# Other steps for raw weight loads, projection rows and one attention half in an attention and feed-forward block on one Trainium2 core

## The chip, the cores and the metric

The kernel runs on one core of a Trainium2 chip. The metric is the device time of one execution in microseconds (us); the time before is the median of three runs. The engines are named as in the profile: PE (TensorE, matrix products; PEld are its weight loads), DVE (VectorE), ACT (ScalarE), POOL (GpSimd) and SP (SyncE, which here issues nearly all transfers).

## What is computed

The input x is 4 sequences of 1024 rows of 512 numbers. Each row is normalised, and the result goes into an attention with decaying weights and into a feed-forward part; both are added to x. Cut to what matters:

```python
xn = _layernorm(x)
# attention: 16 heads of 32, in chunks of T = 128 rows
h = _rmsnorm(xn, qkv_norm_w, eps)
q, k, v = split(h @ _weight_quant(qkv_w).T)
def step(S, qkv_c):
    scores = einsum('bhtd,bhsd,hts->bhts', qi, ki, mask)
    intra = einsum('bhts,bhsd->bhtd', scores, vi)
    cross = einsum('bhtd,ht,bhde->bhte', qi, lam_t, S)
    kv = einsum('bhtd,ht,bhte->bhde', ki, lam_rev, vi)
    return lam_T * S + kv, scale * (intra + cross)
out = _rmsnorm(_rmsnorm(outs, norm_w, 1e-6), proj_norm_w, eps) @ _weight_quant(proj_w).T
# feed-forward, hidden size 2048
gated = silu(xn @ w_gate.T) * (xn @ w_up.T)
x = x + out + gated @ w_down.T
```

`_weight_quant` rounds the weights of the attention to -1, 0 and 1 times a scale that is taken from the mean of their absolute values.

## The kernel before

The 4096 rows are worked on in 8 blocks of 512. Every float32 factor is split into two float16 parts (high and low), so one product is three matmuls. The feed-forward part of block 0 (`ffn0`) prepares the weights as it goes and stores the float16 parts in `gu_d` and `wd_d` in the chip's main memory; block 1 reads them back plainly (`ffn_up`, `load_next` L919); blocks 2 to 7 compute the gate and up products with seven block products in the place of eight (`up_seven`). For these, sums and differences of the raw weights' quarters are needed; `up_sums(i)` makes them once, for i from 0 to 15 (two kinds, gate and up, of eight weight groups).

The feed-forward part is a generator; each `yield` is a step, and 48 steps (`TS`) make a block. The attention runs beside it in 14 + 2 halves of 256 rows: `at[n]` is the step at which half n begins, one every 22 steps, and each of its own `yield`s is placed after one feed-forward step. So PE's order is the order in which the program text emits, and alternates between a feed-forward piece and an attention piece. In a half the first four steps make queries and keys (`psa<-h,wqkT`), the next two the values (`psa<-wvT,h`); after two empty steps come the scores (`pss<-qst,kst`), their products with the values (`psa<-x,t`), the cross terms (`psa<-Sst,qst`) and the state (`psa<-t,kn`); four steps later the projection (`psa<-wpT,x`, 28 steps after the half's begin).

Other engines' work is put into lists by due step (`later`, run by `run_due`) and runs in written order: from step 45 on, `in_order` binds DVE, ACT, POOL and SP each to the order of emission. Before that a scheduler of the framework orders them.

What the change and the steps of the prediction touch:

- `up_sums` L1051: at its step it loads two raw tiles of 256 KB (L1060, `t<-in_w_gu_dram`); two steps later POOL makes four sums (L1070); three and four steps later ACT splits each tile (L1075) and DVE the low part one step on (L1077); five and six steps later SP stores both (L1083, `gu_d<-x`, two transfers of 128 KB for each tile). `sums_at` holds the 16 steps.
- `att_half` with `spread`: queries and keys go through main memory: a store (L634, `sd<-qhl`, `sd<-khl`), then three loads (L643, into `qst` or `kst`) which wait for the store; the keys are also transposed (L637, `kn<-khl`). In steps of the half: query store 2, query loads 3, key store 4, key loads 5; the scores follow at 8.
- `scores` L735: DVE empties the one bank `pss` of the scores. `state` L788: DVE adds the state's bank into `S`. `add_acc` L1142: DVE empties a bank into the accumulator.
- `prep_proj` and `prep_proj_w` (generator `side2`): four tiles of the projection's weights are loaded (L1258), their absolute values summed by ACT and DVE (L297, L299), the scale made (L285 to L293, L332, L333), and each tile turned into -1, 0, 1 (L303, L304 on DVE). It takes one `yield` in each step of its window.
- `moved` and `place`: an estimate of the megabytes moved in each step, by which other transfers (`load_acc`, `load_down`, the stores to `wd_d`, x loads) choose their step inside a window.
- `t32` is a pool of 14 tiles of 256 KB, which raw weights, projection rows and most intermediate results share. PSUM has four banks `psf`, three `psa` and one `pss`.

Of the kernel before, what the change touches and what calls it, by code (L numbers as in the profile page):

```python
# [28 lines left out]
def block_kernel(ctx, tc, x, qkv_w, qkv_nwT, proj_w, proj_nwT, proj_nw, norm_w, s, w_gu, w_down, out):  # L29
# [8 lines left out]
    NB = B * N // HB  # L38
# [21 lines left out]
    def wt(shape, dt, tag, bufs=2):  # L60
        return wk.tile(shape, dt, tag=tag, name=nm(tag), bufs=bufs)
# [28 lines left out]
    def later(steps, *fns, last=False):  # L90

        due[LAST if last else FIRST].setdefault(now[0] + steps, []).extend(fns)

    def run_due(part):
        for fn in due[part].pop(now[0], ()):
            fn()
# [21 lines left out]
    @contextmanager  # L118
    def after(inss):
        with ExitStack() as st:  # L120
            for i in inss:
                st.enter_context(tc.issue_after(i))
            yield
# [41 lines left out]
    def t32():  # L165
        return wt([P, 512], F32, "t32", 14)
# [174 lines left out]
    NG = NJ // 2  # L341
# [100 lines left out]
    def half_scales(hh):  # L442
        gs = slice(hh * NG // 2, (hh + 1) * NG // 2)
        q = wt([P, NG // 2 + 1], F32, "gh2", 1)
        V.tensor_reduce(q[:, 0:1], cg[:, gs], AX.X, ALU.min)
        inverse(c2[:, hh : hh + 1], q[:, 0:1], 1 / XS)
        V.tensor_scalar(q[:, 1:], icg[:, gs], q[:, 0:1], XS, ALU.mult, ALU.mult)
        V.tensor_tensor(bsc[:, gs], bsc0[:, gs], q[:, 1:], ALU.mult)
# [143 lines left out]
    def make_h(b, half):  # L592

        xT = blk[b][0]
        hsl = slice(half * UT, (half + 1) * UT)
        h = wt([P, 2, CC, UT], F16, "h", 1)
        blk[b][1] = h
        th = [t32().rearrange("p (c t) -> p c t", c=2) for _ in range(2)]
        for cp in range(2):
            cs = slice(2 * cp, 2 * cp + 2)  # L600
            G.tensor_tensor(th[cp], xT[:, 0, cs, hsl], xT[:, 1, cs, hsl], ALU.add)

        def split(cp):
            for c in range(2 * cp, 2 * cp + 2):
                t, w = th[cp][:, c % 2, :], nwT[:, c : c + 1]
                A.activation(h[:, 0, c, :], t, AF.Copy, scale=w)
                later(int(b > 0), lambda c=c, t=t, w=w: low(c, t, w), last=True)

        def low(c, t, w):
            V.scalar_tensor_tensor(h[:, 1, c, :], t, w, h[:, 0, c, :], ALU.mult, ALU.subtract)  # L610

        for cp in range(2):
            later(2 + cp if b else 1, lambda cp=cp: split(cp), last=bool(b))
# [437 lines left out]
    def up_sums(i):  # L1051

        g, kind = divmod(i, 2)
        w, ts_ = [], []
        o = om[:, g, kind : kind + 1]

        def load():
            for r in range(2):
                w.append(t32())
                SY.dma_start(w[r], w_gu[2 * g + r, kind])  # L1060

        def sums():
            (a11, a12), (a21, a22) = ([t[:, f * UT : (f + 1) * UT] for f in range(2)] for t in w)
            for dst, a, b, op in (
                (a22, a21, a22, ALU.add),
                (a21, a11, a21, ALU.subtract),
                (a11, a22, a11, ALU.subtract),
                (a12, a12, a11, ALU.subtract),
            ):
                G.tensor_tensor(dst, a, b, op)  # L1070

        def split(r):
            t = wt([P, 2 * C], F16, "x16", 9).rearrange("p (f n q) -> p f n q", f=2, n=2)
            wr = w[r].rearrange("p (f q) -> p f q", f=2)
            A.activation(t[:, :, 0, :], wr, AF.Copy, scale=o)  # L1075
            later(
                1, lambda: V.scalar_tensor_tensor(t[:, :, 1, :], wr, o, t[:, :, 0, :], ALU.mult, ALU.subtract), last=True  # L1077
            )
            ts_.append(t)

        def store(r):
            for f, n in enumerate(((1, 6), (2, 3))[r]):
                SY.dma_start(  # L1083
                    gu_d[:, g, kind, n].rearrange("p n c q -> p (n c q)"),
                    ts_[r][:, f].rearrange("p n q -> p (n q)"),
                )

        load()
        later(2, sums, last=True)
        for r in range(2):  # L1090
            later(3 + r, lambda r=r: split(r), last=True)
            later(5 + r, lambda r=r: store(r))

    def ffn_down(b, hh, gts, c):

# [61 lines left out]
    def ffn(b):  # L1157
        for hh in range(2):
            gts = []
            if b == 1:  # L1160
                js = range(hh * NJ // 2, (hh + 1) * NJ // 2)
                done = plain(gts, js[-4])
                for j in js:
                    yield from ffn_up(b, j, gus.pop(NJ * b + j), bsc, done)
            else:
                for g in range(hh * NG // 2, (hh + 1) * NG // 2):
                    yield from up_seven(b, g, gts)
            yield from ffn_down(b, hh, gts, c2[:, hh : hh + 1])

    def ffn0():  # L1170
        prev = None

        def down(ks):
            g, gts = prev
            for k in ks:
                for _ in ffn_down0(0, k, g, gts, icg[:, g : g + 1]):
                    pass

        for g in range(NG):
            nxt = g + 1 < NG  # L1180
            gts = []
            for r in range(2):
                j = 2 * g + r
                for n, _ in enumerate(ffn_up(0, j, gu0.pop(j), bsc0, plain(gts))):
                    stage(6 * g + 3 * r + n)
                    yield
                if g == 0 and r == 0:
                    load_acc(0, 0)
                    load_acc(0, 1)
                stage(6 * g + 3 * r + 2)  # L1190
                if prev is not None and nxt:
                    down((2 * r, 2 * r + 1))
                    yield
            if not nxt:
                down((0, 1))
                yield
                down((2, 3))
                yield
            prev = (g, gts)
        down((0, 1))  # L1200
        yield
        down((2, 3))
        yield
# [60 lines left out]

    TS = 48
    t0 = [TS * b for b in range(NB)]
    at = [round(36 + 22 * n) for n in range(2 * NB - 2)]
    at += [t0[-1] + 4, t0[-1] + 18]
    mh = {max(t0[b], at[2 * b - 1] + 6) if b else at[0] - 3: (b, 0) for b in range(NB)}
    mh.update({at[2 * b] + (4 if b else 7): (b, 1) for b in range(NB)})  # L1270
# [3 lines left out]
    for n in at:  # L1274
        for i, size in ((2, 1.3), (3, 2.0), (4, 1.3), (5, 2.0), (6, 4.0), (24, 2.0), (25, 2.0)):
            moved[n + i] = moved.get(n + i, 0) + size
    sums_at = [t0[1] + 6 + 3 * i if i < 10 else t0[2] + 1 + 4 * (i - 10) for i in range(2 * NG)]
    for n in sums_at:
        for i, size in ((0, 1.3), (5, 0.7), (6, 0.7)):
            moved[n + i] = moved.get(n + i, 0) + size  # L1280
# [6 lines left out]
    for b in range(1, NB):  # L1287
# [3 lines left out]
        for g in range(NG):  # L1291
            hh, n = divmod(g, NG // 2)
# [10 lines left out]
    t = 0  # L1303
    for b in range(NB):
        if b + 1 < NB:
            ln_plan(b + 1, TS)
        for i, _ in enumerate(ffn(b) if b else ffn0()):
            for _ in range(int(0.9 * max(t - 4, 0)) - int(0.9 * max(t - 5, 0))):
                next(side, 1)
            if 44 <= t < 59:  # L1310
                next(side2, 1)
            if t in mh:
                make_h(*mh[t])
            for n, tn in enumerate(at):
                if tn == t:
                    halves.append(att_half(n // 2, n % 2))
            run_due(LAST)
            for hf in list(halves):
                if next(hf, 1) == 1:
                    halves.remove(hf)  # L1320
            t += 1
            now[0] = t
            if t == 6 * NG - 6:
                SY.dma_start(pnw_bc, proj_nw.partition_broadcast(P))
                V.tensor_scalar(pnw_bc, pnw_bc, ps_sc, None, ALU.mult)
            if b == 0 and i == TS - 1:
                with after(pin):
                    half_scales(0)
                    half_scales(1)
            if b == 0 and i == 44:  # L1330
                in_order(keep=False)
            if t in sums_at:
                up_sums(sums_at.index(t))
            run_due(FIRST)
            run_due(LOADS)
            if b or i > 44:
                in_order()
# [56 lines left out]
```

## Time and profile before

| what | value |
|---|---|
| median of three runs | 1302.11 us (1301.87 to 1303.08) |
| the profiled execution | 1303.48 us |
| its span, first to last instruction | 1301.7 us |
| granted TensorE clock, mean | 0.999 |
| scores, PE `pss<-qst,kst` | 512 matmuls, first at 159.8 us |
| half 1's scores, first | 239.1 us |
| raw weights for the sums, L1060 | 32 loads of 256 KB, first at 183.5 us |
| stores of the sums, L1083 | 64 of 128 KB |

The profile shows one execution. Its page gives each engine's busy time, then the chain of work that ended last, then groups of instructions; the trace behind it can be asked for single stretches. A view of waits lists who waited for whom: the total in us, how often, the longest. A timeline row is: start, duration, engine (SPq is SP's queue), line, operation, output and inputs, number of instructions merged, and in brackets the idle time before it and what ended it. A wait for several things is booked to the one that came last by the records, which for a transfer can be its neighbour in the queue.

### The profile page before, as it was taken

The numbers are of one execution on the slowest core, as the hardware profiler recorded it, in microseconds if no ns is written. First come the engines' busy times: TensorE is split into PE (matmuls) and PEld (weight loads), VectorE is DVE, ScalarE is ACT, GpSimd is POOL, SyncE is SP. The second block draws the span as 40 slices with busy tenths as digits, with TensorE's granted clock in tenths as the row PEclk, the third lists the DMA queues.
The fourth block names the chain that finished last, engine by engine and source line by source line (L and its number), as shares of the span: only waits on it lengthen the run. The fifth ranks groups of instructions, "written<-read, shape, count | busy, mean of one in ns | idle before, by whom it ended". The sixth has DMA issues, their size and how long they took to land.

```text
span 1301.7 us, 26358 instructions
## 1 busy us (share of the span) xinstructions
PE 1264.1 (97%) x10242; PEld 864.5 (66%) x10242; DVE 894.4 (69%) x1603; ACT 609.6 (47%) x1160; POOL 780.4 (60%) x846
## 2 busy tenths in 40 slices
PE   5999999999999999999999999999999999999998
PEld 2444455454785867767677685876858678587684
DVE  7898577666767676747866486755858467777573
ACT  6866635355443454434535254443625336344251
POOL 4535547576687585654947278472846546757273
PEclk9999999999999999999999999999999999999999
DMA  9743755978687796938678676866796776958461
GB/s 342 267 160 113 198 150 151 321 257 248 162 262 272 226 258 155 290 124 255 166 184 289 152 238 154 240 226 175 227 190 189 218 203 202 215 168 254 138 167 49
DMA packets 229950, 268.62 MB, mean 206 GB/s; under 512 B 131520, under 2 KB 156096, under 8 KB 229824
## 3 DMA queue, kind: packets, MB, share of 16 engines
q1 hardware_dynamic: 229680, 266.92, 70.7%
q8 instruction: 80, 1.31, 0.4%
q14 instruction: 46, 0.38, 0.1%
q10 hardware_dynamic: 144, 0.01, 0.0%
HBM read 190.85 MB, written 46.14 MB: 182 GB/s over the span
## 4 chain that ended last, share of the span: by engine, by line
PE 70%; DVE 11%; POOL 6%; ACT 4%; DMA 4%; issue 4%; SPq 0%; DVEq 0%; POOLq 0%; ACTq 0%
PE psf L112 51%; PE psa L112 18%; PE pss L112 2%; POOL t L1070 2%; DMA t<-in_w_gu_dram 1%; DVE h L610 1%; DVE t L986 1%; ACT gu L431 1%; DVE acc L1142 1%; DVE t L735 1%; DMA gu<-gu_d 1%; DVE x L1077 1%; DVE ghl L984 1%; POOL t L740 1%; POOL ghl L946 1%
## 5 line engine op out<-in xcount | busy, mean ns | idle before, releaser
L112 PEld LDWEIGHTS <-gu 128*128 128x128 f16 x3936 | 380.5, 98 | 138.6 <-issue 14.4
L112 PE MATMUL psf<-xT,gu 128*128 128x256 f16 (+1 forms) x1920 | 334.3, 317 | 9.9 <-DVE acc L1142 2.8
L112 PE MATMUL psf<-ghl,ghl 128*128 128x512 f16 x1344 | 306.9, 379 | 1.5 <-POOL ghl L946 0.8
L112 PEld LDWEIGHTS <-ghl 128*128 128x128 f16 x1536 | 146.7, 98 | 164.5 <-POOL ghl L946 3.2
L112 PE MATMUL psf<-wda,gu 128*128 128x256 f16 x2016 | 243.6, 273 | 0.2 <-DVE ghl L984 0.2
L740 POOL TENSOR_TENSOR t<-t,t 128x512 f16<-128x512 f32 x128 | 152.7, 1194 | 147.7 <-ACT t L739 145.2
L735 DVE SCALAR_TENSOR_TENSOR t<-pss,rs,mask 128x512 f32<-128x512 f32 x128 | 95.7, 747 | 66.5 <-PE pss L112 62.5
L739 ACT CAST t<-t 128x512 f16<-128x512 f32 x128 | 78.7, 615 | 122.4 <-DVE t L735 120.6
L1045 POOL TENSOR_TENSOR ghl<-ghl,ghl 128x512 f16<-128x512 f32 x96 | 113.9, 1206 | 21.3 <-ACT ghl L1047 21.3
L112 PE MATMUL psa<-h,wqkT 128*128 128x256 f16 x1024 | 122.3, 273 | 1.3 <-DVE S L788 1.3
L984 DVE SCALAR_TENSOR_TENSOR ghl<-psf,bsc,ghl 128x256 f32<-128x256 f32 x192 | 105.0, 547 | 24.6 <-PE psf L112 11.9
L112 PEld LDWEIGHTS <-wqkT 128*128 128x128 f16 x1024 | 99.8, 98 | 18.9 <-DVE S L788 1.4
L986 DVE TENSOR_TENSOR t<-psf,t 128x256 f32<-128x256 f32 x192 | 93.6, 488 | 18.4 <-PE psf L112 9.7
L702 POOL TENSOR_TENSOR t<-t,t 128x512 f16<-128x512 f32 x28 | 33.3, 1190 | 108.7 <-ACT t L701 86.9
L112 PEld LDWEIGHTS <-wda 128*128 128x128 f16 x864 | 82.9, 98 | 12.2 <-issue 1.1
L811 POOL TENSOR_TENSOR t<-t,nw_bc 128x512 f32<-128x512 f32 x32 | 45.8, 1436 | 55.0 <-DVE t L762 55.0
L112 PE MATMUL psf<-xT,wda 128*128 128x256 f16 x576 | 78.5, 272 | 0.0
L1037 POOL TENSOR_TENSOR ghl<-ghl,t 128x512 f32<-128x512 f32 x48 | 63.9, 1331 | 4.1 <-ACT t L1030 2.1
L686 DVE SCALAR_TENSOR_TENSOR x<-psa,rs,x 128x512 f16<-128x512 f32 x32 | 24.0, 751 | 55.3 <-ACT x L683 53.4
L112 PE MATMUL psa<-wvT,h 128*128 128x512 f16 x256 | 60.5, 379 | 1.3 <-DVE S L788 1.3
L1027 ACT ACTIVATE t<-psf,ug 128x256 f32<-128x256 f32 x48 | 22.7, 473 | 80.4 <-DVE t L986 60.8
L834 POOL TENSOR_TENSOR x<-t,x 128x512 f16<-128x512 f32 x30 | 36.1, 1205 | 40.2 <-ACT x L833 40.2
(220 smaller groups left out, 2012.8 us busy)
## 6 DMA issues: line engine op xcount, KB each, us to landing
gu<-gu_d SPq DMA_DIRECT2D x96, 512.0 KB, 4.2
ghl<-wd_d SPq DMA_DIRECT2D x48, 512.0 KB, 4.8
gu<-gu_d SPq DMA_DIRECT2D x48, 384.0 KB, 3.9
wda<-gu_d SPq DMA_DIRECT2D x48, 384.0 KB, 3.6
qst<-sd SPq DMA_DIRECT2D x48, 256.0 KB, 4.2
kst<-sd SPq DMA_DIRECT2D x48, 256.0 KB, 4.2
t<-in_w_gu_dram SPq DMA_DIRECT2D x44, 256.0 KB, 5.0
t<-in_x_dram SPq DMA_DIRECT2D x32, 256.0 KB, 4.5
```

What stands on the lines that cost most here:

```text
L112: tc.keep_in_program_order(nc.tensor.matmul(*a, **k))
L702: G.tensor_tensor(vrl, vr, vrh, ALU.subtract)
L735: V.scalar_tensor_tensor(sm, pss, u.rk, mask[:, 4 * qd : 4 * qd + 4, :], ALU.mult, ALU.mult)
L739: A.copy(smh, sm)
L740: G.tensor_tensor(sml, sm, smh, ALU.subtract)
L811: G.tensor_tensor(o2, o, nw_bc, ALU.mult)
L834: G.tensor_tensor(on[:, 1, :], u.o3, on[:, 0, :], ALU.subtract)
L984: V.scalar_tensor_tensor(dst, src, by, y, ALU.mult, ALU.add)
L986: V.tensor_tensor(dst, src, y, ALU.add)
L1037: later(2, lambda c_=c_: G.tensor_tensor(c_, c_, us[0][4], ALU.mult))
L1045: G.tensor_tensor(lo[:, f], whole[:, f], hi[:, f], ALU.subtract)
L1070: G.tensor_tensor(dst, a, b, op)
```

## The change

Three things are moved; no computation is added or taken away.

1. `sums_at`: the raw weights of `up_sums` 0 to 4 are loaded at steps 52, 54, 56, 58, 67 in place of 54, 57, 60, 63, 66, and those of 14 and 15 at 111 and 115 in place of 113 and 117; the other nine keep their steps. For 14 and 15 everything after the load is due two steps later than before, counted from the load, so it keeps its step. For 0 to 4 the sums, splits and stores move with their load.
2. `prep_proj` runs in the window of steps 38 to 52 in place of 44 to 58.
3. `at[13]`: attention half 13 begins at step 321 in place of 322.

```diff
         load()
-        later(2, sums, last=True)
+        d = 2 if i >= 14 else 0
+        later(2 + d, sums, last=True)
         for r in range(2):
-            later(3 + r, lambda r=r: split(r), last=True)
-            later(5 + r, lambda r=r: store(r))
+            later(3 + r + d, lambda r=r: split(r), last=True)
+            later(5 + r + d, lambda r=r: store(r))
...
-    at = [round(36 + 22 * n) for n in range(2 * NB - 2)]
+    at = [round(36 + 22 * n) - (n == 13) for n in range(2 * NB - 2)]
...
-    sums_at = [t0[1] + 6 + 3 * i if i < 10 else t0[2] + 1 + 4 * (i - 10) for i in range(2 * NG)]
+    sums_at = [t0[1] + (4, 6, 8, 10, 19, 21, 24, 27, 30, 33)[i] if i < 10 else t0[2] + 1 + 4 * (i - 10) - 2 * (i >= 14) for i in range(2 * NG)]
...
-            if 44 <= t < 59:
+            if 38 <= t < 53:
                 next(side2, 1)
```

Half 1 begins at step 58 (58 = 36 + 22), so its key store and key loads fall on steps 62 and 63. Before, the raw weights of sum 3 are loaded at 63 and those of sum 4 at 66; in the changed kernel sum 3 is at 58 and sum 4 at 67. The estimate `moved` follows `sums_at` and `at`, and with it a few of the placed transfers change their step.

## Prediction

> **What bounds the kernel.** I read the totals and the chain of waits first.
>
> ```profile
> span 1301.7 us, 26358 instructions
> PE 1264.1 (97%) x10242; PEld 864.5 (66%) x10242; DVE 894.4 (69%) x1603; ACT 609.6 (47%) x1160; POOL 780.4 (60%) x846
> PE 70%; DVE 11%; POOL 6%; ACT 4%; DMA 4%; issue 4%; SPq 0%; DVEq 0%; POOLq 0%; ACTq 0%
> ```
>
> TensorE (PE) sets the end: of 1301.7 us it is idle for 1301.7 - 1264.1 = 37.6. The change adds and removes no matmul, so it can only open or close holes in PE. Next, what PE waits for; seven lines of that view:
>
> ```profile
> PE psa L116 <- DVE t L468: 9.8, 3, 9.0
> PE pss L112 <- DMA gu<-gu_d: 4.9, 2, 2.6
> PE psf L112 <- DVE acc L1142: 2.8, 1, 2.8
> ...
> PE psa L112 <- DVE S L788: 2.6, 2, 1.3
> ...
> PE pss L112 <- DVE t L735: 1.7, 2, 1.0
> ...
> PE psf L112 <- DMA xT<-x: 0.4, 1, 0.4
> ...
> PE psf L112 <- DMA ghl<-wd_d: 0.3, 1, 0.3
> ```
>
> The 9.8 is the start, untouched. By windows, the rows that the change can reach are: the two score waits of 4.9 in all (at 157-160 and 236-239 us, attention halves 0 and 1), 2.8 at 416-419, one S L788 wait of 1.3 at 1147, xT 0.4 at 169 and ghl 0.3 at 1126. That is 9.7 us, 0.75% of the span; no gain can be larger.
>
> The score waits are booked to gu loads, but scores read qst and kst. The timeline of SP's queue shows the true one:
>
> ```profile
> 221.05 1.28 SPq L643 DMA_DIRECT2D qst<-sd  x3
> ...
> 225.96 1.42 SPq L634 DMA_DIRECT2D sd<-khl  x1
> 227.43 1.04 SPq L1060 DMA_DIRECT2D t<-in_w_gu_dram  x2
> 228.86 0.88 SPq L1083 DMA_DIRECT2D gu_d<-x  x2
> 232.10 1.27 SPq L643 DMA_DIRECT2D kst<-sd  x3
> ```
>
> The key load is issued when the key store has landed (225.96 + 6.1 to landing = 232.1). Its third part, issued at 232.94, takes 6.1 and lands at 239.0, where PE resumes. The raw weights (L1060) stand between store and load.
>
> **The change part by part.**
>
> *Raw weights of sums 14 and 15, two steps sooner: -2.8.* VectorE's (DVE's) timeline at 416:
>
> ```profile
> 408.73 0.41 DVE L761 TENSOR_TENSOR t<-psa,t 128x256 f32<-128x256 f32 x1
> 409.18 0.42 DVE L762 TENSOR_TENSOR t<-psa,t 128x256 f32<-128x256 f32 x1
> 412.68 2.99 DVE L1077 SCALAR_TENSOR_TENSOR x<-t,om,x 128x512 f16<-128x512 f32 x1 [3.08 <-DMA t<-in_w_gu_dram]
> ```
>
> DVE runs in written order; L1077 of sum 14 holds it for 3.08 us, and behind it stand L735, L1077 and the L1142 that PE waits for. The load was issued at 401.21 to 402.06 and takes 7.0. In the new order it stands two places after the gu load of 392.87, at about 394.4, and waits for no engine, so it lands at 394.9 + 7.0 = 401.9. GpSimd (POOL) ends its previous work at 406.2; four sums end at 409.4, ScalarE's 0.72 makes 410.1, against 412.68: DVE gains 2.6, and L1077 probably not 2.99 but nearer the 1.72 of its successor. So the whole 2.8; between -2.6 and -2.8. SP moves past wda, ghl, out, gu and acc transfers: each two transfers of 256 KB later, about 0.67 each at 390 GB/s, 1.3 in all; in 390 to 425 PE waits for none of them. Without that cover the price is up to 1.3. Sum 15 keeps its steps for all but the load, and in the new order both acc loads come before it, so it lands near 414 as now, in time for its sums at 418.2.
>
> *Half 13 one step sooner: -1.3 and -0.3.* At 1146.36 the twelve state matmuls (psa<-t,kn) are followed at once by half 14's first sixteen (psa<-h,wqkT), which wait for the bank that DVE L788 empties (1147.23, 1.16 us). In the new PE order 24 psf matmuls, 2.6 us by this trace's pitch of 0.109, stand between them: the wait goes. New neighbours are the second projection of half 12 and half 13's first scores; DVE's L1142 (0.75) is the only addition there. The last kst part landed at 1109.25 + 6.9 = 1116.2, 0.3 before its scores; these now come one step (2.6) sooner, but the query store no longer stands behind the x transpose of 1094.15 and the key store follows earlier by more than a step, so I take 0; were it not sooner, the price is 2.6 - 0.3 = 2.3. The ghl wait of 0.3 sits behind the kn transposes of the same half and goes too: between -0.3 and 0.
>
> *Raw weights of sums 0 to 4, clear of half 1's keys: -0.95.* What delays the key load is its store's landing, and in the new order the same transfers precede that store, with one more pair of 128 KB stores. Only the time after 232.1 can shrink: first issue to last landing is 6.9 now. The nearest row for the new situation, two small stores ahead and no raw load, is half 3's kst: 379.84, third issue 381.44, plus 4.4 = 385.8, so 6.0. Gain 0.95; the other end is half 13's 7.7 (1108.41 to 1116.1), a loss of 0.8; the best is all of 2.3. The sums themselves move to 181-220 us. Their cover: POOL idles 3.73 and 4.95 us before its L946 at 189.56 and 195.82, and one sum takes 3.4 to 4.1; DVE loses the projection pieces there. Cost 0; if a load came late there, DVE would be held as at 412.68, up to 2.8.
>
> *Projection rows six steps sooner: +1.2 and +1.0.* Here the new order speaks against the change. The four loads (4 x 0.67 = 2.7) now stand before half 0's query store (139.91); half of one gu load (0.67) moves behind it: +2.0 for its landing at 145.2. The query load, the key store and the key load are chained behind it. One kn transpose, whose landing lies 0.8 after the last query load, moves into the wait: 2.0 - 0.8 = +1.2 on the wait of 2.6. The bounds are +2.0 and -1.1: the store's data was through by 142.4 on fifteen of sixteen engines, and an instruction fetch of 1.85 us beginning at 141.4 made the sixteenth 2.3 us late; if that falls elsewhere, 1.2 - 2.3 = -1.1. Taking proj's loads out of 156-167 might close xT's 0.4, but DVE, next, is late there anyway: 0.
>
> [...]
>
> DVE: scores have one bank (pss), and each L735 must empty it before the next scores. At 168-172 DVE is busy 3.82 of 4.00.
>
> ```profile
> 172.71 0.68 DVE L299 TENSOR_REDUCE asum<-t 128x1 f32<-128x512 f32 x1
> 173.42 0.68 DVE L795 SCALAR_TENSOR_TENSOR Sst<-S,Sst 32x512 f16<-32x512 f32 x1
> 174.13 0.75 DVE L735 SCALAR_TENSOR_TENSOR t<-pss,rs,mask 128x512 f32<-128x512 f32 x1
> ```
>
> L735 ends at 174.88; the next scores start at 175.56, a margin of 0.68. In the new order L299 (0.68) is gone from here, and in come the five scale pieces (188.75 to 189.46: 0.71) and one L303 + L304: 0.48 + 0.75 at 195.0, or 0.59 + 1.64 at 197.0. Net 0.71 + 1.23 - 0.68 = 1.26 up to 2.26; less the margin, PE waits 0.6 to 1.6. The mean of L303 + L304 is 1.9, so 1.2; part of the delay runs beside the later kst, and I take +1.0 of 0 to 1.6. At the following scores one more L303 + L304 replaces an L299, and the margin there holds.
>
> The dear row, 1.64, ran beside POOL's L811 and L1070. [...]
>
> *Sum:* -2.8 - 1.3 - 0.3 - 0.95 + 1.2 + 1.0 = -3.15. The profiled execution took 1303.48 (1301.7 of span, 1.8 around it); 1300.3 follows. The median of the runs shown, 1302.11, lies 1.37 lower: 1299.0.
>
> **The rivals.**
>
> A, *the opening is free*: proj's loads and DVE work fit, both +1.2 and +1.0 drop: -5.35, 1296.8. For it: PE had only 0.4 of waits between 160 and 236, and the bounds reach 0. Against: DVE's 3.82 of 4.00.
>
> B, *the keys' load is bound by its store, and the move does not do what it says*: no 0.95 but +0.8, the rest as above: -1.4, 1300.7. For it: the raw loads stand behind the store, not ahead. Against: half 3's row.
>
> C, *slower: the opening pays twice*. The 2.7 of row loads delay the query pair in full and, without a drain, the key pair again; the instruction fetch's 2.3 falls on the second store too, and DVE adds 1.6: 2.7 + 2.7 + 2.3 + 1.6 = 9.3, against the gains of 5.35: +3.95, 1306.1. It decides once the opening costs over 5.35 + 2.6 = 8. For it: query and key transfers are one chain, in one queue. Against: the DMA engines were nearly idle from 142.4 to 146.
>
> **How the numbers follow.** About 0.2%, 2.6 us, is what a measurement of this kernel tells from no change: faster is below 1299.5, slower above 1304.7. Chances: forecast 0.40, A 0.27, B 0.18, C 0.15. The forecast lies 0.5 from the bound; most of its error is on the side of its large, well-founded terms, so 0.32 of its 0.40 is faster: 0.32 + 0.27 = 0.59. Same: 0.08 + 0.18 = 0.26. Slower 0.15. Without C the ends of the bounds are -2.8 - 1.3 - 0.3 - 2.3 - 0.4 - 1.1 = -8.2 and -2.6 - 1.3 + 0.8 + 2.0 + 1.6 = +0.5, or +2.8 with half 13's 2.3. All at an end together is unlikely: 1295.0 to 1304.0 leaves out C and a few in a hundred of A.
>
> **What would show it.** In the profile after: no PE wait for DVE acc near 416; no PE wait for S L788 near 1147, its other one, 1.3 near 1218, unchanged; half 1's first-key-issue to last landing near 6.0 and a score wait of about 1.4 there; the first score wait nearer 3.8 than 2.6; a new PE wait for DVE L735 near 175-178. Wrong would be: the DVE hold by L1077 appearing at another place, a score wait at half 0 under 1.5 or over 6, or any wait over 1 us near 1085-1140.

## The result: slower, and the profile after

| | median, us | executions |
|---|---|---|
| before | 1301.91 (1301.65 to 1303.08) | 5 |
| after | 1308.14 (1306.41 to 1310.41) | 5 |
| after / before | 1.0047, 95% interval 1.003 to 1.0064 | |

The same pair was measured again later, beside more executions: 1306.91 against 1304.02, ratio 1.0026 (1.0015 to 1.0037). So the change costs some 3 us (3.4 by this ratio, 2.9 between the medians), and the 6.2 of the first measurement come in part from a low draw of before, whose medians in four later groups of 17 to 34 executions are 1303.1 to 1304.0. The forecast was 1299.0, faster.

The page of after: its head, the row of PE and the engines' shares of the chain that ended last.

```profile
span 1308.5 us, 26358 instructions
...
PE 1267.8 (97%) x10242; PEld 865.6 (66%) x10242; DVE 892.4 (68%) x1603; ACT 610.0 (47%) x1160; POOL 779.8 (60%) x846
...
PE 74%; DVE 9%; POOL 5%; ACT 4%; DMA 4%; issue 3%; SPq 0%; DVEq 0%; POOLq 0%; ACTq 0%
```

The span grew by 6.8. PE idles for 1308.5 - 1267.8 = 40.7 where it idled for 37.6: 3.1 of the 6.8. The other 3.7 stand in PE's *busy* time, with the same 10242 matmuls: they ran slower. The mean granted clock is 0.994, and was 0.999. Next PE's waits in after (who waited for whom: total in us, times, longest):

```profile
PE pss L112 <- DMA gu<-gu_d: 4.9, 1, 4.9
PE pss L112 <- DVE t L735: 3.3, 4, 1.0
PE psf L112 <- DMA ghl<-wd_d: 3.2, 2, 2.7
...
PE psa L112 <- DVE h L610: 1.4, 2, 1.0
PE psa L112 <- DVE S L788: 1.3, 1, 1.3
```

The total of the first row is that of before, 4.9, but it was two waits and is one: half 0's first scores wait for all of it, half 1's hardly (0.4, booked elsewhere). L735 was 1.7 in two waits and is 3.3 in four. The 2.8 for DVE's acc at 416 is gone, and 3.2 for the down weights (`ghl<-wd_d`) has come, 2.7 of it near 404. One of the two waits for S L788 is gone, and L610 has taken its place. Most of what the change freed came back under another name.

Where the clock went is in the view by windows, cut at the borders of the half-speed stretches that the trace records, which are 3.41 us long or twice that (columns: window, its length, PE busy, granted clock, DMA share, GB/s, with other engines between):

```profile
157.26:160.67 3.41, 1.92 (x9) 0.69 (x7) 3.41 (x7) 2.23 (x5) 1.92 (x2) 1.00 0.79 184
160.67:164.09 3.42, 0.04 (x1) 0.07 (x2) 0.03 (x1) 0.00 (x0) 0.00 (x0) 1.00 0.96 223
164.09:167.50 3.41, 3.41 (x12) 1.48 (x13) 1.81 (x4) 1.66 (x3) 1.16 (x1) 0.50 1.18 293
...
403.02:406.44 3.42, 0.80 (x7) 0.44 (x6) 1.89 (x3) 2.68 (x5) 3.42 (x3) 1.00 1.02 378
406.44:409.85 3.41, 3.29 (x8) 1.16 (x8) 2.13 (x2) 1.88 (x3) 3.04 (x4) 0.50 1.00 305
```

Half 0's score wait leaves the window from 160.67 empty, and in the next PE is granted 0.50: it does in 3.41 us what takes 1.7 at full speed (0.50 x 3.41). The wait near 404 is followed by the same, with 0.80 busy in one window and 0.50 granted in the next. Between the first clock record of its trace, at 20.7, and the last stretch, after has four such windows (27.6, 102.7, 164.1, 406.4); before, from 22.3 on, has one (100.8). Two of the four don't belong to the change: 27.6 lies ahead of all that was moved, and no_rows and rows_loads_far, which are no slower than before, have it too; and after_again, the same kernel once more, has no window near 406, and its longest wait there is 0.7. The one at half 0's scores is there both times.

### The profile page after: what moved, and what is told of

Its sections match the earlier page's. It is cut to its first block, busy times and chain, and to the rows that moved or that the text cites. A ratio compares the mean times of both kernels' runs of the same rounds, so it can differ in the third digit from the quotient of the medians.

```text
span 1308.5 us, 26358 instructions
## 1 busy us (share of the span) xinstructions
PE 1267.8 (97%) x10242; PEld 865.6 (66%) x10242; DVE 892.4 (68%) x1603; ACT 610.0 (47%) x1160; POOL 779.8 (60%) x846
## 4 chain that ended last, share of the span: by engine, by line
PE 74%; DVE 9%; POOL 5%; ACT 4%; DMA 4%; issue 3%; SPq 0%; DVEq 0%; POOLq 0%; ACTq 0%
PE psf L112 54%; PE psa L112 18%; PE pss L112 2%; DMA gu<-gu_d 1%; ACT gu L431 1%; DVE t L735 1%; POOL t L1070 1%; DVE acc L1143 1%; DVE ghl L984 1%; DVE h L610 1%; DVE t L986 1%; DMA t<-in_x_dram 1%; ACT t L435 1%; DMA sd<-qhl 1%; POOL ghl L946 1%
## 5 line engine op out<-in xcount | busy, mean ns | idle before, releaser
L112 PE MATMUL psf<-ghl,ghl 128*128 128x512 f16 x1344 | 310.0, 382 | 4.4 <-DMA ghl<-wd_d 3.2
L735 DVE SCALAR_TENSOR_TENSOR t<-pss,rs,mask 128x512 f32<-128x512 f32 x128 | 95.7, 748 | 73.2 <-PE pss L112 70.2
L112 PEld LDWEIGHTS <-wqkT 128*128 128x128 f16 x1024 | 99.8, 98 | 19.3 <-issue 1.8
L811 POOL TENSOR_TENSOR t<-t,nw_bc 128x512 f32<-128x512 f32 x32 | 45.8, 1436 | 57.1 <-DVE t L762 57.1
L502 DVE TENSOR_TENSOR x<-t,x 128x512 f16<-128x512 f32 x52 | 52.7, 1020 | 11.1 <-ACT x L500 10.8
```

Source lines behind the costliest of these rows:

```text
L112: tc.keep_in_program_order(nc.tensor.matmul(*a, **k))
L502: lambda: V.tensor_tensor(xn2[:, 1, :], src, xn2[:, 0, :], ALU.subtract),
L735: V.scalar_tensor_tensor(sm, pss, u.rk, mask[:, 4 * qd : 4 * qd + 4, :], ALU.mult, ALU.mult)
L811: G.tensor_tensor(o2, o, nw_bc, ALU.mult)
```

## The experiments

All kernels were timed in five rounds beside before. "Clock" is what half-speed windows took from an execution on average: (1 - granted clock) x span; for before it is 2.7 to 3.2 in the four groups.

| kernel | ratio to before | 95% interval | clock, us |
|---|---|---|---|
| half13_alone | 0.9986 | 0.9973 to 0.9999 | 2.0 |
| sums14_alone | 0.998 | 0.9967 to 0.9992 | 2.3 |
| sums0_alone | 1.0003 | 0.9992 to 1.0014 | 2.5 |
| rows_alone | 1.0034 | 1.0017 to 1.005 | 4.6 |
| after_again | 1.0026 | 1.0015 to 1.0037 | 4.4 |
| no_rows | 0.9989 | 0.9976 to 1.0003 | 1.5 |
| half13_sums14 | 0.9989 | 0.9974 to 1.0004 | 2.1 |
| half13_sums14_one | 0.9976 | 0.9961 to 0.9991 | 1.6 |
| the same kernel again (half13_one_far) | 0.9967 | 0.9954 to 0.9981 | 2.2 |
| rows_filled | 1.0051 | 1.0032 to 1.0071 | 2.4 |
| rows_loads_only | 1.0022 | 1.0007 to 1.0037 | 4.0 |
| rows_loads_far | 0.9989 | 0.9976 to 1.0002 | 2.4 |
| rows_far_work_soon | 0.9997 | 0.9985 to 1.0008 | 1.8 |
| best_far | 0.9958 | 0.9942 to 0.9974 | 0.9 |

The intervals are as wide as most of the effects. So each profile was also cut at fixed points of PE's order (half 0's first query matmul, the first score matmuls of halves 0, 1, 2, 5 and 8, and the last matmul), and stretches between them compared. This is worked out from the start times in the traces, in us; * marks a stretch with a half-speed window.

| kernel | query 0 to scores 0 | scores 0 to 1 | 1 to 2 | 2 to 5 | 8 to end |
|---|---|---|---|---|---|
| before | 33.96 | 79.29 | 76.55 | 220.49 | 544.42 |
| half13_alone | 31.16 | 78.78 | 76.55 | 220.12 | 543.49 |
| sums14_alone | 32.93 | 79.00 | 76.55 | 220.28 | 544.13 |
| sums0_alone | 32.84 | 79.59 | 78.24* | 221.45* | 545.08 |
| rows_alone | 35.89 | 80.08* | 76.55 | 220.40 | 544.47 |
| after | 36.20 | 80.57* | 76.55 | 222.44* | 543.48 |
| after_again | 35.66 | 80.75* | 76.71 | 220.02 | 543.51 |
| no_rows | 33.07 | 79.26 | 76.55 | 219.05 | 543.47 |
| half13_sums14 | 32.56 | 79.52 | 78.24* | 219.07 | 543.50 |
| half13_sums14_one | 31.29 | 79.01 | 76.55 | 218.85 | 543.51 |
| rows_loads_only | 36.45* | 80.24* | 76.55 | 220.75 | 545.62 |
| rows_loads_far | 31.16 | 79.01 | 76.56 | 219.79 | 544.00 |
| rows_far_work_soon | 31.16 | 79.73 | 76.56 | 224.46* | 544.42 |
| best_far | 31.16 | 79.76 | 78.05* | 218.42 | 543.51 |

The column "1 to 2" gives the price of one half-speed window by itself: 76.55 without and 78.24 with one, so 1.69. A single row is one execution, and a draw: without any edit near it, the last column runs from 544.00 to 545.62.

**Each part alone.** First half 13:

```diff
-    at = [round(36 + 22 * n) for n in range(2 * NB - 2)]
+    at = [round(36 + 22 * n) - (n == 13) for n in range(2 * NB - 2)]
```

> Only the start of half 13, one step sooner; the rest as before. Theory 1 (the parts' PE waits add up as the trace of after shows them): the waits at 1126 (0.4) and 1147 (1.4) go, two of 0.6 and 1.2 on DVE's h take their place one step later, and the last stretch gains 0.9 in all as it does in after (from 7.2 behind at 1154 to 6.5 behind at 1225): -0.9, nothing else moves. Rival (granted clock): what decides is how many windows of 3.4 us run at half speed, and since this edit touches no long wait it leaves the time within 0.5 of before or, if the windows fall otherwise, at a multiple of 1.7 from it.

The last column falls from 544.42 to 543.49, and is 543.47 to 543.51 in all eight kernels of the study with this edit: -0.93 against before, as theory 1 had it, and 0.5 to 2.1 against the other kernels without the edit. Its PE waits from 1080 on are:

```profile
PE psa L112 <- DVE h L610: 1.5, 2, 1.0
PE psa L112 <- DVE S L788: 1.3, 1, 1.3
PE psf L112 <- DVE t L986: 0.7, 1, 0.7
```

The S L788 wait at 1147 is gone, but half 14's query matmuls, which stood behind it, now run into the low part of their own input (`h`, L610), which DVE makes just then. The profile also shows no score wait at half 0, where before has 2.6: its query store landed 3.35 after its issue, where it took 5.29 in before. That is no part of the edit (more on it below).

Sums 14 and 15:

```diff
+        d = 2 if i >= 14 else 0
-        later(2, sums, last=True)
+        later(2 + d, sums, last=True)
...
-    ... else t0[2] + 1 + 4 * (i - 10) for i ...
+    ... else t0[2] + 1 + 4 * (i - 10) - 2 * (i >= 14) for i ...
```

> Only the raw weights of sums 14 and 15 loaded two steps sooner. Theory 1: the hold of DVE at 412 and PE's 2.8 at 416 go, but the load of the down weights (ghl<-wd_d) that PE needs at 403 of after's time lands 2.7 later because the raw loads share its engines, so that PE waits 2.9 there and 0.6 at 420: +0.6 in all with no half-speed window, +2.3 with one. Rival (the late down weights come from half 3's later key chain in after, so from the other parts): no wait for wd_d here, the 2.8 is gained: -2.8.

Its PE waits between 390 and 425 are one row:

```profile
PE psf L112 <- DMA ghl<-wd_d: 2.5, 3, 1.1
```

So the wait has changed its name, as theory 1 says, with a stretch of 220.28 against 220.49; but the time fell by 2.6, as the rival says. Both are met in part: the wait of 2.8 is replaced by three of at most 1.1, and no half-speed window follows the three short ones here. Theory 1's reason isn't what the trace shows: the first down weights take 6.7 from issue to landing here and took 6.9 in before, so the raw loads don't slow them (more on it below). Among the eight kernels that keep the old steps, three show such a window in this stretch; of five with two steps sooner, one (after, where most of the wait for the down weights is in one piece).

Sums 0 to 4:

```diff
-    sums_at = [t0[1] + 6 + 3 * i if i < 10 else ...
+    sums_at = [t0[1] + (4, 6, 8, 10, 19, 21, 24, 27, 30, 33)[i] if i < 10 else ...
```

> Only the raw weights of sums 0 to 4 loaded at other steps. Theory 1: half 1's score wait falls from 2.45 to about 0.6 as in after, first key issue to last landing from 6.9 to about 5.6: -1.9, and -1.7 more where that wait used to cost a half-speed window. Rival (in after half 1's wait shrank because half 0 had already made PE late): the wait stays within 0.5 of 2.3 and the time within 0.5 of before.

No gain. SP's timeline of this kernel in front of half 1's scores, which begin at 238.0:

```profile
225.88 0.95 SPq L919 DMA_DIRECT2D gu<-gu_d  x2
226.93 0.42 SPq L634 DMA_DIRECT2D sd<-khl  x1
227.44 1.19 SPq L1083 DMA_DIRECT2D gu_d<-x  x2
231.81 1.27 SPq L643 DMA_DIRECT2D kst<-sd  x3
```

The raw loads are gone from between store and load, and the key load takes 6.0 from first issue to last landing in place of 6.9. But the wait is 2.1 against 2.3. From half 1's first query matmul PE takes the same 34.8 to its scores in every trace, the wait aside; what has moved is the key load, issued 30.6 after that matmul and not 30.0. And before's 6.9 is the longest of the six kernels with the sums and the rows at their old steps (6.1 to 6.9), whose waits are 1.2 to 2.3: against these no gain shows, here or in no_rows (5.8, with a wait of 1.6).

Nor did half 1's wait shrink in after because PE came late from half 0. In rows_loads_only (further down) PE is as late there, and half 1's wait is 1.5; rows_alone, with the sums where before has them, shows 0.1, and rows_far_work_soon, not late at half 0, 0.6. It is the rows' work, done sooner, that goes with the short wait. The rival's number holds, its reason doesn't.

The projection rows:

```diff
-            if 44 <= t < 59:
+            if 38 <= t < 53:
                 next(side2, 1)
```

> Only the projection rows' loads and their work, six steps sooner. Theory 1: the query store lands 2.7 later, half 0's score wait grows from 2.8 to 5.0 (+2.2), two waits on DVE L735 of 0.9 come (+1.8), xT's 0.5 goes, and a wait of 5 us fills a whole window of the clock, so that the next 3.4 us run at half speed (+1.7): +5.2, and half the profiles show one more half-speed window than before. Rival (granted clock by chance, the rows are cheap): +1.2 and +1.0 as predicted, so at most +2.2 in PE waits, and the rest of the loss of after is not here.

1.0034: the loss of after. The two windows at half 0's wait:

```profile
157.62:161.03 3.41, 0.00 (x0) 1.00 1.03 227
161.03:164.44 3.41, 3.00 (x11) 0.50 1.16 287
```

(Columns: window, length, PE busy, clock, DMA share, GB/s.) PE has nothing to do for a whole window, and half the clock, 0.50, in the next.

**Do they add, and is it the rows?** The changed kernel again, and after with the rows put back:

> The changed kernel once more, on the chip and beside the runs of before that the other kernels of this call use. The parts alone gave ratios of 0.9986, 0.998, 1.0003 and 1.0034. Theory 1 (they add): 1.0003, at 1304.4. Rival (they spoil one another: the rows make PE and half 3's keys late, so that sum 14's raw loads meet the down weights): 1.0045, near 1310.

> The changed kernel with one part undone: the projection rows at their old steps, the other three parts as in after. Theory 1 (the rows are the whole loss): as half 13 with sums 14 and 15, whose ratio is 0.9989, times 1.0003 of sums 0 to 4: 0.999, 1302.6; half 0's score wait back at 0.2 to 2.8, none on L735 near 180 to 190. Rival (the other parts lose as well once they are together): 1.000 to 1.0015.

The product of the parts is 1.0003, and after measures 1.0026. The four intervals together make the product uncertain by some 0.0027, so this doesn't tell whether the parts add. Taking the rows out of after brings it from 1.0026 to 0.9989. What is left of the other three, 0.11%, has an interval that holds no change.

**Which half of the rows' edit costs: the loads or the work?** Loads at step 38 and work from step 48 on, as before (`for _ in range(10)` in place of 4 between the loads and `prep_proj_w`, window 38 to 58):

> The four row loads six steps sooner, but the work on them on VectorE, ScalarE and GpSimd at its old steps. Theory 1 (the loads make the score wait, the work makes the two L735 waits): score wait 4.7 to 5 and a half-speed window after it as with the rows alone, the L735 waits at 178 to 190 gone (-1.75): ratio 1.0034 less 0.0013 = 1.002. Rival (the L735 waits come from PE's arriving late in a row of work fixed on DVE, whichever work it is): they stay, 1.0034.

Its PE waits from 140 to 240:

```profile
PE pss L112 <- DMA gu<-gu_d: 5.1, 1, 5.1
```

No L735 wait is left, and the score wait is all there (half 1's begins after 240): theory 1. The loads cost 2.9 us, of which 1.1 is clock (4.0 against 3.0).

Then the loads at step 34, four steps further ahead of the query store (`range(14)`, window 34 to 58):

> The four row loads ten steps sooner, so that three transfers and some 6 us more lie between them and half 0's query store; the work on them at its old steps. Theory 1 (what costs is to stand right ahead of the store, not to be early): store lands in 3.4 to 5.3 as in before, score wait 0.2 to 3.0 by where the instruction fetch falls, xT's wait smaller since its transposes no longer stand behind the rows: -0.5 to 0 in waits, ratio 0.999 to 1.000. Rival (any 1 MB more in that stretch costs, wherever it stands): 1.002 as with the loads six steps sooner.

0.9989, and half 0's score wait is gone. SP's timeline of this kernel, and below it that of rows_alone:

```profile
135.28 0.33 SPq L634 DMA_DIRECT2D sd<-qhl  x1
135.89 1.07 SPq L919 DMA_DIRECT2D gu<-gu_d  x2
138.29 1.28 SPq L643 DMA_DIRECT2D qst<-sd  x3
...
147.96 1.26 SPq L643 DMA_DIRECT2D kst<-sd  x3
```

```profile
138.19 2.09 SPq L1258 DMA_DIRECT2D t<-in_proj_w_dram  x4
140.38 0.38 SPq L634 DMA_DIRECT2D sd<-qhl  x1
...
147.50 1.29 SPq L643 DMA_DIRECT2D qst<-sd  x3
...
155.05 1.25 SPq L643 DMA_DIRECT2D kst<-sd  x3
```

The query load can be issued when the store has landed: 138.29 - 135.28 = 3.0 without the rows right ahead, 147.50 - 140.38 = 7.1 with them, for the same 512 KB. One more thing differs: the store itself is issued 4.6 to 5.1 sooner, because ACT's copy of the second query bank (L662) runs at 133.95 and not at 138.58. Up to step 45 the framework's scheduler orders the engines, and with other loads it chose another order. So the wait may be gone for two reasons. The 3.0 is counted from the issue, so its being earlier is not in it, but it may hang in part on an instruction fetch, which starts 7.7 after the store's issue here and 2.7 after it in rows_alone (last section).

And the work six steps sooner, with the loads out of the way (`range(8)`, window 34 to 52):

> The four row loads ten steps sooner, as in the kernel whose ratio was 0.9989, and the work on them six steps sooner, as in after. Theory 1 (the earlier work costs the two L735 waits of 0.9, whatever the loads do): they are there, half 0's score wait stays at 0.2, and the time is 1.75 above that kernel: ratio 1.0002. Rival (the L735 waits come only where PE is late from the score wait, with DVE's work bunched behind it): no such waits, 0.9989 again.

PE's waits from 140 to 240:

```profile
PE pss L112 <- DVE t L735: 1.5, 2, 0.9
PE psf L112 <- DMA xT<-x: 0.7, 1, 0.7
PE pss L112 <- issue: 0.6, 1, 0.6
```

The two L735 waits are there with no score wait ahead of them, so they belong to the work. By the column "scores 0 to 1" they cost 79.73 - 79.01 = 0.7, and not their 1.5: PE comes later to half 1's scores, whose wait falls from 1.6 to 0.6. The ratios, 0.9997 and 0.9989, fit that, but their intervals overlap.

**Is the half-speed window a matter of PE's idle time?** rows_alone with further matmuls in the wait:

```diff
             pss = bank(ps_s, (P, 4, P))
+            if u.g == 0 and qd == 0:
+                for _ in range(28):
+                    T.matmul(pss[:, 0:2, :], wqkT[:, 0, 0:P], hhi[:, 0, :], start=True, stop=True)
```

> The rows six steps sooner, as in the kernel with these alone, and 28 further matmuls of 256 columns (28 x 0.109 = 3.05 us of PE work, their results overwritten) in front of half 0's first scores, in the wait of 4.7. Theory 1 (an idle of more than some 1.8 us within one window of 3.4 us halves the clock in the next): the wait shrinks to 1.6, no half-speed window follows it, and the kernel is faster than with the rows alone by 1.7 although it computes more: 1306.2, ratio 1.002. Rival (half-speed windows do not hang on PE's idle time): same as the rows alone, 1.0034, with a half-speed window near 161 all the same; if the 3.05 lay on the path, 1.0057.

The clock answers as theory 1 says: the loss falls from 4.6 to 2.4, and the windows at half 0 are

```profile
157.46:160.88 3.42, 1.81 (x17) 1.00 1.07 238
160.88:164.29 3.41, 2.79 (x16) 1.00 1.18 268
```

The time doesn't: 1309.07, above rows_alone. The filler isn't on the path (the last key part lands at 161.30 there and at 161.24 in rows_alone; scores start 0.2 later in both), but PE, now at full speed, meets the next late transfer, xT, for 1.3 at 172, which eats most of the 1.7. The rest of the loss stands far behind, in waits that are longer than in rows_alone or missing there (1.9 at 324, where rows_alone has 0.8; 0.8 at 831; 0.6 at 1123; 0.7 at 1134, where it has 0.3). Why 28 more matmuls at 157 should bring those, no run shows.

**Towards a better kernel.** The two parts that gain, and the same with sums 14 and 15 only one step sooner:

> Half 13 a step sooner and the raw weights of sums 14 and 15 two steps sooner; the rows and sums 0 to 4 as before. Theory 1 (they add): 0.9986 x 0.998 = 0.9966, 4.4 us faster than before. Of it 2.2 in PE's waits, the rest in half-speed windows (the 2.8 at 416 gone as one wait). Rival (the gain of sums14 alone was clock by chance): the waits for ghl<-wd_d, 3.0 in its profile, eat the 2.8, and half 13's 0.9 alone is left: 0.9993 to 0.9986.

> As the kernel with half 13 and sums 14 and 15, but these loads only one step sooner than before. Theory 1: with one step the down weights of step 111 stand ahead of sum 14's raw weights again, so the waits for ghl<-wd_d near 396 to 411 fall from 3.0 to under 1, while the raw weights land some 4 sooner than in before, still enough for DVE: 1.5 to 2.5 better than with two steps, 0.995 of before. Rival (one step is not enough): DVE's hold comes back with 1 to 2.8 at 416, and the time is that of half 13 alone, 0.9986.

> Half 13 a step sooner and the raw weights of sums 14 and 15 one step sooner once more, beside the others of this call: 0.9976 was measured with an interval of 0.9961 to 0.9991. Theory 1: the same again, 0.9965 to 0.998, as the waits at 413 fell from 2.8 to 0.9 and 0.6 without a half-speed window. Rival: that gain was luck with the windows, and it is the 0.9986 of half 13 alone.

(The last label misleads: it is the second measurement of half13_sums14_one, with nothing moved among the rows.) One step is better than two by the traces: the wait for DVE's acc at 416 stays at 0.5 or less, and the stretch from scores 2 to 5 is 218.85, and 218.96 in the second measurement, where two steps give 219.05 to 220.28, and 222.44 with a half-speed window. The ratios lean the same way, with intervals that overlap. Last, with the rows' loads at step 34:

> Half 13 a step sooner, the raw weights of sums 14 and 15 one step sooner, the row loads ten steps sooner with their work at its old steps, sums 0 to 4 as before. Theory 1 (the parts add): 0.9972 (the mean of its two measurements without the row loads) x 0.9989 = 0.9961. Rival (they overlap, since in the first kernel's profiles half 0's score wait was 0.3 by a lucky instruction fetch): 0.9972.

0.9958, 1298.07 against 1303.09: faster than before and after. Its interval holds the sum of the parts, 0.9961, and the rival's 0.9972 as well, so whether the row loads add their share stays open. With no long wait left at half 0 or at 416 the clock takes 0.9 only.

## Why the prediction was wrong, point by point

Nearly every sign that the prediction named for itself is in the profile of after: no wait for DVE's acc near 416, none for S near 1147, a key load near 6.0, a longer first score wait, new waits for L735. The time went the other way all the same, because of what stands behind the signs.

**The rows' score wait, +1.2: mis-sized, and its half-speed window left out.** The step's mechanism, the row loads standing in front of the query store and the chain behind it, is what the runs show. Its size is off in three places. First, counted from half 0's first query matmul, the store was to land 2.0 later; in the five kernels with the rows there it lands 2.4 to 3.2 later than in before (21.8 to 22.5 against 19.3), being issued 0.6 to 1.0 later and taking 6.7 to 7.7 from issue to landing, against 5.3. And the saving of 0.8 by the kn transpose moved ahead doesn't arise, since the key store, now issued 1.4 after the query loads, lands only behind their data (6.1 in place of 4.8, rows_alone). The wait is 4.3 to 5.1 in these kernels, without the filled one; 3.8 was forecast. The second place is the base: before's 5.29 was already a slow one. In the eight kernels with the rows at their old steps it takes 3.35 to 5.5, in step with where an instruction fetch falls. The working saw that fetch, but took the draw of one profile for the rule; by the column "query 0 to scores 0" the stretch grows from 32.4, the mean of those eight (half13_one_far, not in the table, has 31.25), to 36.1, the mean of the four unfilled kernels with the rows ahead: 3.7. Third, no term of the sum held the clock: a wait of 5 us fills most of a window of 3.4 wherever it falls, and the clock takes 1.1 to 1.5 more than in before in rows_alone, after_again and rows_loads_only. Being early is not what costs: the same loads at step 34 give 0.9989, with an interval that holds 1, and at step 38 1.0022.

**VectorE's work, +1.0: near in sum.** It came as two waits of 0.7 and 0.9, not one. The first has the cheap row, 0.48 + 0.75, for which the working had 0.6. At the following scores the margin didn't hold, as an L304 took 1.53 and an L303 2.24 there. Both ran beside POOL operations that had begun before them (at 182.81 for 1.28, and from 185.62 to 187.76), as the dear row of before did (1.64 from 197.62, beside an L811 of POOL that began at 197.26); the L304 of 0.75 ran beside none. No run moves these POOL operations alone, so that they are the cause is not shown. Half 1's wait gave back part, so that 0.7 is left (rows_far_work_soon).

**Sums 14 and 15, -2.8: the step that failed is "in 390 to 425 PE waits for none of them".** The hold by L1077 went, as forecast. But now PE waits for down weights. SP's timeline of after:

```profile
397.95 0.38 SPq L929 DMA_DIRECT2D gu<-gu_d  x1
398.37 0.43 SPq L1120 DMA_DIRECT2D ghl<-wd_d  x1
398.90 0.85 SPq L1083 DMA_DIRECT2D gu_d<-x  x2
...
400.89 1.30 SPq L1060 DMA_DIRECT2D t<-in_w_gu_dram  x2
...
409.42 4.61 SPq L1155 DMA_DIRECT2D acc<-in_x_dram  x2
414.11 0.89 SPq L1083 DMA_DIRECT2D gu_d<-x  x2
415.10 0.41 SPq L1120 DMA_DIRECT2D ghl<-wd_d  x1
```

In before one load of the accumulator (L1154, here L1155) stands on each side of these last down weights; with the new `moved` both are placed ahead. The second can't be issued until the store `out_dram<-acc` has landed, and SP's queue stands behind it: in all five kernels with two steps that hold is 3.4 to 4.6, and the last down weights are issued 18.1 to 20.6 after half 3's first scores. With one step the hold is 1.5 to 1.6 and the issue at 15.6 to 16.6; with the old steps no load of the accumulator waits for that store, and the issue is at 14.1 to 16.4. The working saw that both loads come first, and asked only what that does to the raw weights behind them. PE waits for down weights, 1.4 to 3.2 in sum with two steps, 0.7 to 1.3 with one; with the old steps for 0.2 at most, but for one kernel with 1.7 (rows_far_work_soon), so they are close to late in any case. "Up to 1.3" as the price of that cover was taken from the transfers' own length, without asking how close they stood to being late.

The longest of these waits, 2.7 near 404 in after, is a draw: the down weights of 398.37 land after 8.15, in after_again after 6.04, and PE doesn't wait for them there. Their like take 6.0 to 6.9 in thirteen of the 16 traces and 7.75 to 8.15 in three, one with each order of the raw loads. Without half-speed windows the stretch from scores 2 to 5 is 220.3 with the old steps (mean of five), 219.6 with two (four) and 218.7 with one (three): of the 2.8, two steps gained 0.7 and one step 1.6.

**Sums 0 to 4, -0.95: nothing.** The key load was forecast at 6.0 and took 6.0 in sums0_alone and 5.6 in after. The step that failed is that only the time after the load's issue can change: it is issued 0.6 later in sums0_alone, seen from PE's own work, and the 6.9 it was measured against was the longest of six. Rival B had the place right.

**Half 13, -1.6: -0.93.** Both waits went. What was missed is the next thing late, DVE's L610 behind the neighbour that the wait had hidden: it could have been read in the order of DVE around 1150.

With these sizes the sum is 3.7 + 0.7 + 1.5 for the clock - 0.7 + 0 - 0.9 = +4.3, an estimate from single traces, between the 2.9 and the 6.2 that were measured.

**The rivals.** C's time, 1306.1, was the nearest, and two of its mechanisms are there (the query pair delayed, DVE 1.6). But its point of decision, an opening that costs over 8, is not what happened: the stretches to half 0's and half 1's scores together cost 3.5 in after's profile against before's, clock included, and 5.1 against the mean of the eight kernels with the rows at their old steps. The loss came because most of the gains of 5.35 weren't there to pay for it; that C's number is the nearest is in part luck.

## What to carry to other kernels

A transfer may be early in its queue and still be in the wrong place: don't put bytes that nobody needs soon right ahead of a store that a load waits for; the four loads gave 1.0022 there, and cost nothing that can be measured when issued four steps further ahead (0.9989, 0.9976 to 1.0002). In a queue that issues in order, ask of every transfer that moves what it waits for, and who then stands behind it: here one load of the accumulator held SP's queue for 3.4 to 4.6. When a wait is removed, look up what is needed next behind it and how close that is to late, in the same stretch of the trace: the 2.8 at 416 gave way to 2.5 for down weights in sums14_alone. And a base read off one execution may be a draw, as before's 5.29 was among landings of 3.35 to 5.5: compare the same stretch in several.

## What the runs showed of the hardware that was not expected

*In these traces the half-speed windows go with the idle time in one window, not with the longest wait.* The borders of the half-speed stretches lie in every trace on one raster of 3.413 us (after's begin at 27.56, 102.65, 164.09 and 406.44, which is 22, 18 and 71 times 3.413 apart), whose phase differs from execution to execution (before's begins at 100.83). In the 16 traces, between the first clock record and the last stretch, no window with less than 1.78 us of PE idle was followed by one at half speed (in before 1.76, from 237.36 on, was not); all twelve with 2.03 or more were (in after 3.38 from 160.67 and 2.62 from 403.02; one of the twelve was itself at half speed, in rows_loads_only, which ran two such windows in a row); between these, 13 of 19 (among them 1.98 from 97.42 in before, and 1.78 from 24.14 and 1.98 from 99.24 in after). So with the 1.69 of above, a wait of 2.0 in one window can cost 1.7 more, while the 2.8 split over two, with 1.60 and 1.21 idle, costs nothing more in before at 416 (same columns as above; the next window, from 421.68, is granted 1.00):

```profile
414.86:418.27 3.41, 1.81 (x16) 0.90 (x15) 3.38 (x5) 0.62 (x1) 1.47 (x3) 1.00 0.23 79
418.27:421.68 3.41, 2.20 (x21) 1.97 (x21) 3.36 (x6) 0.37 (x1) 3.17 (x4) 1.00 0.41 127
```

*Half 0's query store landed later where an instruction fetch fell early in it.* In the eight kernels with the rows at their old steps, half 0's query store of 512 KB takes 3.35 to 3.40 to land where a fetch of 16 KB (0.9 to 1.9 us) starts 2.8 to 2.9 after its issue, in three of them, and 4.55 to 5.5 where it starts 1.5 to 1.9 after, in five. The time from the matmul before to half 0's first scores is 0.2 to 0.3 in the first case and 1.6 to 3.0 in the second. Where no fetch starts within 7.5 of the issue, in the three kernels with the row loads at step 34, it takes 3.0. No run moves the fetch alone, so that it is the cause is argued and not shown.
